# First blocks of a causal self-attention: turned probability tiles laid four to a PSUM bank and copied by whole banks

## The chip, the cores and the metric

The kernel runs on one core of a Trainium2 chip, in one launch. The metric is the device time of that core in microseconds (us): the median of several executions. The engines of a core work side by side, each through its own queue in order, and wait for each other by semaphores: TensorE (PE in the profile, PEld for its weight loads), VectorE (DVE), ScalarE (ACT), GpSimd (POOL) and SyncE (SP, which issues the DMAs). TensorE writes its results to PSUM, which here is eight banks of 128 partitions by 512 float32 values; VectorE and ScalarE take them out of there into SBUF.

## What is computed

The reference is one layer of an encoder and a decoder in float32: model width 512, 16 heads of 32, feed-forward width 2048. The encoder works on 2 x 77 context rows, the decoder on 2 batches of 2048 tokens. Its self-attention is causal, with a bias by relative position:

```python
y = tgt
yn = _ln(y, dec_n1_s, dec_n1_b)
y = y + _mha(yn, yn, dec_sa_in_w, dec_sa_in_b, dec_sa_out_w, dec_sa_out_b, sb)
y = y + _mha(_ln(y, dec_n2_s, dec_n2_b), memory, dec_ca_in_w, dec_ca_in_b, dec_ca_out_w, dec_ca_out_b, cb)
h = _ln(y, dec_n3_s, dec_n3_b)
y = y + (jax.nn.relu(h @ dec_ff1_w.T + dec_ff1_b) @ dec_ff2_w.T + dec_ff2_b)
```

Inside `_mha`, for each head: scores = q k^T / sqrt(32) + bias, softmax over the keys, times the values. `sb` is the bias with minus infinity above the diagonal.

## The kernel before

**Units and visits.** Self-attention is cut by batch `b` (2), block `m` of 512 queries (4), group `g` of four heads (4) and tile `t` of 128 queries (4). One such unit is a row of queries against the key tiles 0 to `i = 4m + t`, so a unit has `i + 1` key tiles of 128. The list `stream` cuts each unit into pieces of up to four key tiles; a visit is one round of the main loop (lines 1811 to 1841), which takes one or two pieces of the same unit. In a first block (`m == 0`) a unit has 1, 2, 3 or 4 key tiles, hence one piece and one visit.

**What a visit issues**, in this order:

- `turn` (lines 412 to 436): the probabilities of the four heads are turned on PE by transposes of 128 x 128 (L426), into a PSUM bank that `bank()` hands out. When a bank has its load, one copy takes it to a buffer of the ring `pts_all` (eight buffers): on ACT (L433) or on DVE (L431). In a first block the loads go by head: four loads, each with the 1 to 4 key tiles of one head. Loads with an even number go to ACT, odd ones to DVE. At the end, `exps` puts the exponentials (L406) of a later unit into ACT's queue.
- `slot(n + 1)`, when the unit ends here: side work for PE and the rest. In first blocks these are projections of q (L215), k (L226 or L1068) and v (L239 or L1068) with their evictions (L217, L231, L242, L1075 to L1093), norms that are turned (L305, taken out by L310 on ACT or L312 on DVE), and stages of another part: in batch 0 the encoder (L577 to L764; among them its scores L606, with the row maxima L616 and sums L627 on DVE), in batch 1 the cross-attention of the very first block (L810 to L882; among them its scores L835 and sums L853).
- `score_next`: the scores of a later unit (L375), four heads into four banks. DVE takes them out (L384 far from the diagonal, L391 with the bias near it), keeping maxima in `mx`; L401 makes the negative row maximum `nm`, for which the exponentials wait.
- `values`: for each key tile and head one matmul of the turned probabilities with the values (L455). It reads the copies in `pts`. In a first block all four tiles of a group add into one bank, which is kept out of the list of banks from the first of them to the last, and is then copied by ACT (L466).

**Banks.** `bank()` hands out the eight banks (seven while one is kept) in a fixed round: the bank just handed out goes to the end of the list. All users draw from the same list: turns, scores, projections, turned norms, side stages. A matmul that writes a bank waits until the engine that empties it has done so.

Of the kernel before, what the change touches and what calls it, by code (L numbers as in the profile page):

```python
# [22 lines left out]
HC = P // HD  # L23
MB = 512
NMB = T // MB
TB = MB // P
# [28 lines left out]
def tile_encoder_decoder(ctx: ExitStack, tc: tile.TileContext, ins, out):  # L55
# [103 lines left out]
    with (  # L159
# [20 lines left out]
        def bank():  # L180

            ring.append(ring.pop(0))
            return psum[:, ring[-1], :]

        def in_turn(what, tile):
            i = count[what] % tile.shape[1]
            count[what] += 1
            return tile[:, i, :]
# [163 lines left out]
        def exps(k):  # L352

            for _ in range(min(k, len(late_exps))):
                late_exps.pop(0)[1]()
# [56 lines left out]
        def turn(pieces):  # L412

            first = units[pieces[0][0]][1] == 0
            loads = []
            for n, k0, kn in pieces:
                ks = range(k0, k0 + kn)
                if first:
                    loads += [[(n, k, r) for k in ks] for r in range(HC)]
                else:  # L420
                    loads += [[(n, k, r) for r in range(HC)] for k in ks]
            for o, load in enumerate(loads):
                pt = bank()
                pts = in_turn("pts", pts_all).rearrange("p (x q) -> p x q", q=P)
                for x, (n, k, r) in enumerate(load):
                    nc.tensor.transpose(pt[:, ts(x, P)], state[n]["p"][r][:, k], ident)  # L426
                    got[n, k, r] = pts[:, x, :]
                w = len(load) * P
                free = pieces[0][0] == len(units) - 2 and pieces[0][1]
                if free or (o % 2 if first else o in (4, 6) if len(loads) == 8 else o >= (len(loads) + 1) // 2):  # L430
                    nc.vector.tensor_copy(pts[:, : len(load), :], pt[:, :w])  # L431
                else:
                    nc.scalar.copy(pts[:, : len(load), :], pt[:, :w])  # L433
                if not first and o == (7 if len(loads) == 8 else min(3, len(loads) - 1)):
                    exps(1)
            exps(HC if first else 0 if units[pieces[0][0]][1] == NMB - 1 else 1)
# [1374 lines left out]
        while i < len(stream):  # L1811
            n = stream[i][0]
# [3 lines left out]
            while any(u == n for u, _ in late_exps):  # L1816
                exps(1)
            ends = pair[-1][1] + pair[-1][2] == size[n]
            turn(pair)
            if n == end - 2:  # L1820
                for _, k0, _ in pair:
# [88 lines left out]
```

## Time and profile before

| | us |
|---|---|
| median of 3 runs | 2738.47 |
| lowest, highest | 2737.07, 2738.86 |
| the profiled execution | 2739.13 |
| its span, first to last instruction | 2737.3 |

| engine | busy us | share of the span | instructions |
|---|---|---|---|
| PE | 2711.1 | 99% | 26462 |
| DVE | 1821.8 | 67% | 5338 |
| ACT | 1539.9 | 56% | 2996 |
| POOL | 991.1 | 36% | 836 |

The granted TensorE clock was 0.999 over the span. The first blocks lie at about 26 to 160 us (batch 0) and 860 to 996 us (batch 1). In these stretches:

```
28.00:160.00 132.00, 126.20 (x1054) 78.54 (x1053) 91.92 (x347) 62.61 (x184) 47.63 (x37) 1.00 0.62 182
860.00:996.00 136.00, 133.46 (x1040) 85.03 (x1030) 90.11 (x340) 74.42 (x214) 46.20 (x41) 1.00 0.46 133
```

The columns are the stretch, its length, the busy time (and number of instructions) of PE, PEld, DVE, ACT and POOL, the granted clock, the share of the DMA engines and GB/s.

How to read the rows further below. A group of instructions has its line, engine, operation, tiles out<-in, shapes and count; then busy us, mean ns of one, and the idle time of the engine before it with what ended it. A row of the timeline has start, length, engine, line, operation and, in brackets, the idle time before it and its releaser. A row of the chain of waits has start, length and what the time is put down to. Matmuls are pipelined: their starts are closer together than their lengths, so what counts for PE is the distance between starts. A wait is put down to the semaphore that came last; an engine is named there that may only have finished at the same moment.

### The profile page before, as it was taken

The page shows a single profiled execution, that of the slowest core. Times are in us where ns is not written, and L with a number is a line of the kernel's source. Part 1 is how long each engine was busy: PE and PEld are TensorE (multiplying, and loading weights), DVE is VectorE, ACT ScalarE, POOL GpSimd, SP SyncE. Part 2 cuts the span into 40 slices and gives each one's busy share as a digit, 9 for nine tenths or more (in the row PEclk, how much of TensorE's full clock was granted, in tenths as well). Part 3 has the DMA queues.
Part 4 walks back from the last instruction along what each step waited for, and adds up shares of the span by engine and source line. Part 5 has one row for each costly group of instructions (what it writes and reads, how often), then busy time and mean ns, then how long its engine had stood idle before and what let it go on. Part 6 is the DMA issues. An engine that isn't in the chain of part 4 may idle for free.

```text
span 2737.3 us, 67718 instructions
## 1 busy us (share of the span) xinstructions
PE 2711.1 (99%) x26462; PEld 2182.6 (80%) x26462; DVE 1821.8 (67%) x5338; ACT 1539.9 (56%) x2996; POOL 991.1 (36%) x836
## 2 busy tenths in 40 slices
PE   9999999999999999999999999999999999999998
PEld 5578777777776677777777887898989898989898
DVE  5776687787875587687787793646464746464645
ACT  3554567767786557667777785444444444444431
POOL 1512234500210513313300103465646564646456
PEclk9999999999999999999999999999999999999999
DMA  7624345511212522333311206565758565756465
GB/s 225 182 86 133 121 126 176 161 55 41 63 48 72 147 75 71 108 111 106 128 44 33 64 19 225 166 220 166 219 166 242 165 219 166 220 166 220 150 224 185
DMA packets 293666, 377.47 MB, mean 138 GB/s; under 512 B 39984, under 2 KB 163936, under 8 KB 293218
## 3 DMA queue, kind: packets, MB, share of 16 engines
q1 hardware_dynamic: 293346, 373.12, 44.3%
q8 instruction: 210, 3.44, 0.5%
q14 instruction: 110, 0.90, 0.1%
HBM read 328.38 MB, written 44.64 MB: 136 GB/s over the span
## 4 chain that ended last, share of the span: by engine, by line
PE 94%; ACT 2%; DVE 2%; issue 1%; POOL 0%; DMA 0%; SPq 0%; ACTq 0%; DVEq 0%; POOLq 0%
PE psum L426 18%; PE psum L1556 14%; PE psum L1585 12%; PE psum L375 11%; PE psum L455 9%; PE psum L1068 8%; PE psum L215 4%; PE psum L1719 3%; PE psum L1676 3%; PE psum L865 2%; ACT pp L406 1%; PE psum L835 1%; PE psum L873 1%; PE psum L589 1%; PE psum L810 1%; PE psum L239 1%
## 5 line engine op out<-in xcount | busy, mean ns | idle before, releaser
L406 ACT ACTIVATE pp<-pp,nm 128x128 f32<-128x128 f32 (+15 forms) x512 | 611.9, 1201 | 30.1 <-DVE nm L401 29.6
L384 DVE TENSOR_SCALAR_CACHE_REDUCE pp<-psum 128x512 f32<-128x512 f32 (+3 forms) x1024 | 556.4, 591 | 56.2 <-PE psum L375 53.7
L433 ACT COPY pts<-psum 128x512 f32<-128x512 f32 (+2 forms) x732 | 383.6, 580 | 277.0 <-PE psum L426 224.8
L426 PE MATMUL psum<-ident,pp 128*128 128x128 f32 x4352 | 527.6, 276 | 9.7 <-ACT nT L310 4.5
L426 PEld LDWEIGHTS psum<-ident,pp 128*128 128x128 f32 x4352 | 471.4, 140 | 67.1 <-DVE pp L384 24.0
L375 PE MATMUL psum<-kT,q 32*128 32x512 f32 (+3 forms) x2560 | 331.7, 560 | 2.8 <-ACT nT L310 1.6
L455 PEld LDWEIGHTS psum<-pts,vv 128*32 128x32 f32 x8704 | 226.6, 110 | 126.5 <-DVE pp L384 47.0
L431 DVE COPY pts<-psum 128x512 f32<-128x512 f32 (+3 forms) x404 | 251.6, 654 | 94.5 <-PE psum L426 92.5
L1585 PE MATMUL psum<-pp 128*128 128x128 f32 x2560 | 304.5, 276 | 1.9 <-POOL pp L961 1.6
L1585 PEld LDWEIGHTS psum<-pp 128*128 128x128 f32 x2560 | 296.3, 192 | 8.6 <-issue 3.0
L455 PE MATMUL psum<-pts,vv 128*32 128x128 f32 x8704 | 278.8, 275 | 0.7 <-DVE mx L391 0.3
L961 POOL TENSOR_TENSOR pp<-pp 128x512 f32<-128x512 f32 x159 | 212.9, 1356 | 121.0 <-DMA pp<-in_dec_ff_wT_dram 45.4
L1556 PE MATMUL psum<-vv,pp 128*128 128x256 f32 x1024 | 236.2, 381 | 0.0
L375 PEld LDWEIGHTS psum<-kT,q 32*128 32x128 f32 x2560 | 142.1, 183 | 106.7 <-issue 42.0
L1556 PEld LDWEIGHTS psum<-vv,pp 128*128 128x128 f32 x1024 | 190.3, 190 | 25.8 <-issue 0.5
L391 DVE CUSTOM_DVE_ANT_0 pp<-psum,bias 128x256 f32<-128x256 f32 (+1 forms) x512 | 196.0, 411 | 20.9 <-PE psum L375 20.8
L1569 DVE TENSOR_TENSOR kT<-kT,psum 128x512 f32<-128x512 f32 x96 | 65.8, 686 | 191.1 <-PE psum L1556 190.9
L1572 ACT ACTIVATE kT<-kT,vecs 128x256 f32<-128x256 f32 x192 | 87.1, 501 | 156.6 <-DVE kT L1569 155.9
L1556 PE MATMUL psum<-nT,pp 128*128 128x256 f32 x768 | 174.1, 380 | 0.0
L1556 PEld LDWEIGHTS psum<-nT,pp 128*128 128x128 f32 x768 | 144.2, 190 | 20.3 <-issue 1.6
L1593 ACT COPY oT<-psum 128x128 f32<-128x128 f32 x56 | 15.0, 268 | 238.8 <-PE psum L1585 238.8
L493 POOL TENSOR_TENSOR oT<-rirows,oT 128x512 f32<-128x512 f32 x30 | 38.4, 1279 | 288.5 <-DMA rirows<-rec 239.9
(257 smaller groups left out, 4049.3 us busy)
## 6 DMA issues: line engine op xcount, KB each, us to landing
pp<-w_d SPq DMA_DIRECT2D x520, 256.0 KB
pp<-in_dec_ff_wT_dram SPq DMA_DIRECT2D x112, 256.0 KB
wqk<-in_dec_sa_in_wT_dram SPq DMA_DIRECT2D x76, 256.0 KB
bias<-tzg SPq DMA_DIRECT2D x128, 128.0 KB
pp<-wo_d SPq DMA_DIRECT2D x56, 256.0 KB
vv<-in_enc_ff_wT_dram SPq DMA_DIRECT2D x8, 1024.0 KB
xr<-in_x_dram SPq DMA_DIRECT2D x32, 256.0 KB
vv<-y SPq DMA_DIRECT2D x32, 256.0 KB
```

The lines of the kernel that those rows point to most:

```text
L375: nc.tensor.matmul(banks[r][:, : kn * P], q[rows4(r), ts(t, P)], kT[rows4(r), g, k0 * P : (k0 + kn) * P], start=True, stop=True,)
L384: nc.vector.tensor_scalar(p[:, k0 : k0 + far], s[:, :far], 1.0, None, ALU.mult, ALU.max, accum_out=st["mx"][:, r, c : c + 1],)
L391: nc.vector.tensor_tensor_reduce(p[:, k0 + far : i + 1], s[:, far:kn], near[:, 2 - (kn - far) :], 1.0, LOWEST, ALU.add, ALU.max, accum_out ...
L406: nc.scalar.activation(p, p, AF.Exp, bias=nm, accum_out=to)
L426: nc.tensor.transpose(pt[:, ts(x, P)], state[n]["p"][r][:, k], ident)
L431: nc.vector.tensor_copy(pts[:, : len(load), :], pt[:, :w])
L433: nc.scalar.copy(pts[:, : len(load), :], pt[:, :w])
L455: nc.tensor.matmul(ot[rows4(r)], vv[:, k, ts(g * HC + r, HD)], got.pop((n, k, r)), start=k == k0 and (whole or not begun), stop=k == k1 - ...
L961: engine.tensor_tensor(out, a, b, ALU.subtract)
L1068: nc.tensor.matmul(mm[:, ts(f, TOK)], left[:, c, ts(f, P)], right[:, c, :], start=c == 0, stop=c == 1,)
L1556: nc.tensor.matmul(mm[:, ts(f, TOK)], a[:, c, ts(f, P)], b[:, c, :], start=fresh and f == 0 and c == 0, stop=c == 1, skip_group_check=True,)
L1585: nc.tensor.matmul(psum[:, bank_i, ts(col, P)], lhs[:, c, :], w[:, c, :], start=fresh and k in (0, 3) and c == 0, stop=c == 3, skip_group_ ...
```

## The change

In `turn`, for first blocks, the loads are no longer one for each head. The turned tiles of a visit are put in one list, head after head, and cut into loads of `TB` = 4:

```diff
                 if first:
-                    loads += [[(n, k, r) for k in ks] for r in range(HC)]
+                    heads = [(n, k, r) for r in range(HC) for k in ks]
+                    loads += [heads[o : o + TB] for o in range(0, len(heads), TB)]
                 else:
                     loads += [[(n, k, r) for r in range(HC)] for k in ks]
```

A visit with 1, 2 or 3 key tiles so has 1, 2 or 3 loads of four tiles instead of 4 loads of 1, 2 or 3 tiles; with 4 key tiles the loads are the same as before. Each load still takes one bank, one buffer of `pts_all` and one copy, even ones on ACT, odd ones on DVE. The transposes keep their order, and the value matmuls theirs.

## The prediction

> **What bounds the kernel now.** I read the page first, then the waits of PE in the two stretches of first blocks (26 to 160 us for batch 0, 860 to 996 us for batch 1), then the timeline and the chain of waits around each of those waits.
>
> ```profile
> span 2737.3 us, 67718 instructions
> ...
> PE 94%; ACT 2%; DVE 2%; issue 1%; POOL 0%; DMA 0%; SPq 0%; ACTq 0%; DVEq 0%; POOLq 0%
> ```
>
> PE carries the chain. What other engines do counts only where PE stands still, so the first question is how long it does in the stretches that the change touches. The waits of PE (who waits, for whom, total us, times, longest), batch 0 first:
>
> ```profile
> PE psum L426 <- ACT nT L310: 3.2, 2, 1.8
> PE psum L426 <- DVE mx L391: 1.1, 2, 0.7
> PE psum L375 <- ACT kT L231: 0.7, 1, 0.7
> PE psum L426 <- ACT pts L433: 0.6, 1, 0.6
> ```
>
> ```profile
> PE psum L426 <- DVE kT L1081: 1.0, 1, 1.0
> ```
>
> Together 6.6 us, the first rows of both answers, nearly all of it at L426: transposes that wait for a PSUM bank in which an older result still stands. That is the most that better use of banks can win directly; every matmul stays as it is.
>
> **The change part by part.** A group of four heads has four visits with 1, 2, 3 and 4 key tiles; two batches of four groups make 8 visits of each size. The fourth is unchanged. The first three make 3 x 4 copies and take as many banks now, and 1 + 2 + 3 = 6 afterwards. Transposes and value matmuls keep their number. The copies, by shape, in 28 to 160 us:
>
> ```profile
> L431 DVE COPY pts<-psum 128x512 f32<-128x512 f32 x8 | 5.3, 686 | 2.9 <-PE psum L426 2.9
> L433 ACT COPY pts<-psum 128x512 f32<-128x512 f32 x8 | 4.7, 586 | 13.1 <-PE psum L426 12.5 <-DVE pts L431 0.6
> ...
> L431 DVE COPY pts<-psum 128x384 f32<-128x384 f32 x8 | 4.1, 548 | 0.0
> L433 ACT COPY pts<-psum 128x384 f32<-128x384 f32 x8 | 3.8, 478 | 12.8 <-PE psum L426 12.0 <-ACT pts L433 0.6
> L433 ACT COPY pts<-psum 128x256 f32<-128x256 f32 x8 | 3.0, 373 | 14.9 <-PE psum L426 14.7
> L431 DVE COPY pts<-psum 128x256 f32<-128x256 f32 x8 | 3.0, 415 | 0.0
> L431 DVE COPY pts<-psum 128x128 f32<-128x128 f32 x8 | 1.9, 280 | 0.0
> L433 ACT COPY pts<-psum 128x128 f32<-128x128 f32 x8 | 1.8, 272 | 1.8 <-PE psum L426 1.8
> ```
>
> Even loads go to ACT, odd ones to DVE. ACT per group: 2 x (0.272 + 0.373 + 0.478) = 2.25 us now, (1 + 1 + 2) x 0.586 = 2.34 us afterwards. DVE: 2 x (0.280 + 0.415 + 0.548) = 2.49 us now, (0 + 1 + 1) x 0.686 = 1.37 us afterwards. Over eight groups ACT does 0.8 us more and DVE 8.9 us less. By itself that is no time: PE sets the end. I cost it at nothing except where a copy stands in the chain, which comes below.
>
> What can move time is which bank a step is given. The list hands out the bank whose last use lies furthest back, so 3, 2 and 1 fewer banks a visit mean that everything after is given an older, more surely emptied bank. I went through the list by the code for both batches, and took at each wait of PE the step that will own the new bank. First the pace of turns without a wait, for 4 and 12 transposes:
>
> ```profile
> 123.28 0.66 PE L426 MATMUL psum<-ident,pp 128*128 128x128 f32 x4
> 123.77 1.89 PE L1068 MATMUL psum<-xt,wqk 128*128 128x256 f32 x8
> ...
> 140.87 1.53 PE L426 MATMUL psum<-ident,pp 128*128 128x128 f32 x12
> ...
> 142.24 1.02 PE L597 MATMUL psum<-vv,pp 128*77 128x512 f32 x2
> ```
>
> The next matmul starts 0.49 us after the first of 4 and 1.37 us after the first of 12: 0.11 us for each transpose, so 0.93 us for 8.
>
> Batch 0, first group, second and third visit:
>
> ```profile
> 33.96 0.88 PE L426 MATMUL psum<-ident,pp 128*128 128x128 f32 x6
> ...
> 35.17 0.41 PE L426 MATMUL psum<-ident,pp 128*128 128x128 f32 x2 [0.34 <-DVE mx L391]
> ...
> 35.64 3.70 PE L226 MATMUL psum<-nT,wqk 128*128 128x512 f32 x8
> ...
> 41.45 1.70 PE L426 MATMUL psum<-ident,pp 128*128 128x128 f32 x12
> ...
> 42.12 0.42 DVE L391 CUSTOM_DVE_ANT_0 pp<-psum,bias 128x256 f32<-128x256 f32 x1
> ...
> 43.29 1.12 PE L239 MATMUL psum<-wbig,nT 128*128 128x512 f32 x2
> ```
>
> The fourth bank of the first turn held head 0's scores. Its two new banks held nothing newer than the visit before. L226 could start at 33.96 + 0.93 = 34.89: 0.75 us won. In the next visit L239 waits for head 1's scores; afterwards it gets the bank of head 0, emptied at 42.54 by the DVE row, so it starts at 41.45 + 1.37 = 42.82: 0.47 us more.
>
> Batch 0, third group, first visit, and batch 1, last group, first visit:
>
> ```profile
> 95.63 0.55 PE L426 MATMUL psum<-ident,pp 128*128 128x128 f32 x3
> ...
> 96.89 0.30 PE L426 MATMUL psum<-ident,pp 128*128 128x128 f32 x1 [0.71 <-DVE mx L391]
> ...
> 97.14 3.70 PE L226 MATMUL psum<-nT,wqk 128*128 128x512 f32 x8
> ```
>
> ```profile
> 961.72 0.44 PE L426 MATMUL psum<-ident,pp 128*128 128x128 f32 x2
> ...
> 963.12 0.67 PE L426 MATMUL psum<-ident,pp 128*128 128x128 f32 x2 [0.97 <-DVE kT L1081]
> ...
> 963.85 1.32 PE L1068 MATMUL psum<-xr,wqk 128*128 128x256 f32 x5
> ```
>
> One bank instead of four: neither turn meets the bank it waits for. 97.14 - (95.63 + 0.49) = 1.02 us and 963.85 - (961.72 + 0.49) = 1.64 us won.
>
> Two waits go without gain. The 0.6 us at L426 in batch 0's second group vanishes, but the chain passes it by:
>
> ```profile
> 79.29 1.43 DVE emx L616
> ...
> 83.71 2.93 ACT pp L406 x8
> 86.64 0.58 ACT kT L231
> ...
> 87.26 0.50 PE psum L375 x8
> ```
>
> DVE and the exponentials set when L375 may start; PE only waits 0.87 us longer there. And the largest, L310 (3.2 us, two waits), stays: the second load of those turns still gets the bank of the turned norm tile that ACT empties behind four exponentials. There the change has a price:
>
> ```profile
> 108.20 1.20 PE L426 MATMUL psum<-ident,pp 128*128 128x128 f32 x9 [1.41 <-ACT nT L310]
> ...
> 109.15 0.48 ACT L433 COPY pts<-psum 128x384 f32<-128x384 f32 x1 [0.65 <-ACT pts L433]
> ...
> 109.53 0.72 ACT L406 ACTIVATE pp<-pp,nm 128x512 f32<-128x512 f32 x1
> ...
> 110.64 0.86 PE L455 MATMUL psum<-pts,vv 128*32 128x128 f32 x24
> ```
>
> ACT's second copy needs 8 transposes after the release instead of 6, 2 x 0.11 us, and is 0.586 - 0.478 = 0.11 us longer. The exponentials behind it, then L310, then the next turn are late by 0.33 us. The value matmuls at 110.64 are not: the copy ends near 110.0. This is the shortest cover of a copy; elsewhere whole projections or encoder stages, as L597 at 142.24, lie between the transposes and L455.
>
> Last, in batch 1's last group the chain runs through DVE's copies themselves:
>
> ```profile
> 977.90 0.93 DVE pts L431 x2
> ```
>
> One copy of 0.69 us there: 0.24 us won.
>
> Sum: 0.75 + 0.47 + 1.02 + 1.64 + 0.24 - 0.33 = 3.8 us. Against the profiled execution, 2739.13 us (span 2737.3 and 1.8 around it), that is 2735.3; that execution lies 0.7 us over the median of 2738.47, so I predict 2734.7 us. After each block PE runs nearly without waits (94% of the chain), so I carry the gain to the end whole; the bounds are nothing carried, and the waits of ACT won as well (rival b).
>
> **The rivals.** (a) *Swallowed.* Each freed wait returns as at 87.26, since DVE or ACT sets the next release. For it: a third of the waits shown behave so. Against: the chain shows PE straight after L226 and L1068. Time: 2738.47 - 0.24 = 2738.2.
>
> (b) *More waits go than I credit.* If DVE's 8.9 us less work and the earlier PE also shorten the ACT waits (3.2 + 0.7 + 0.6 us), 3.8 + 4.5 = 8.3 us are won: 2730.2. For it: DVE stands in the chain at 79.29 and keeps PE at 96.89. Against: those waits end with exponentials that wait for row maxima, and these come before the copies in DVE's order.
>
> (c) *Slower: the late copy delays ACT.* ACT starts a copy only when four transposes are in, and the exponentials queue behind it. By the pace (0.27 us for the first transpose, 0.11 for each more), ACT leaves a first visit's copies at 0.61 + 0.59 = 1.20 us instead of 0.49 + 0.27 = 0.76, and a third visit's at 1.48 + 0.59 = 2.07 instead of 1.15 + 0.48 = 1.63; a second visit's stay. 0.88 us a group, 7.0 us in eight: 2745.5. It decides only where the row maxima are ready before the copies end and PE then waits for ACT; the trace has this once (109.53). [...]
>
> **How the numbers follow.** The forecast has 0.48, (a) 0.12, (b) 0.30, (c) 0.10. A measurement of this kernel tells about 0.2%, 5.5 us, from no change: faster means below 2733.0, slower above 2743.9. All of (b) and an eighth of the forecast's spread are faster, 0.36; of (c) 0.07 is slower; the rest, 0.57, is the same. The range reaches to (b)'s end and past (a): 2730.0 to 2740.0, which leaves out (c) and a deeper (b). The forecast's own range is 2732 to 2737.
>
> **What would show it.** The copies at L431 and L433 fall by 48 in number, all with 128x512 in first blocks. PE's waits at L426 for L391 and for L1081 are gone; those for L310 stay, the second 0.3 us longer. L375's wait for L231 grows to about 1.5 us. PE between 860 and 996 us wins more than between 26 and 160. Wrong would be: a wait at L455 for pts; exponentials released by L433 instead of L401; or any change of more than 1 us after 1000 us, where nothing is touched.

## The result and the profile after

| kernel, set of runs | runs | median us | lowest, highest |
|---|---|---|---|
| before | 15 | 2737.40 | 2735.83, 2738.86 |
| changed, same set | 15 | 2731.85 | 2730.52, 2734.27 |
| changed, second set (before 2737.83) | 11 | 2734.49 | 2732.18, 2736.75 |
| changed, third set (before 2737.87) | 11 | 2734.60 | 2731.46, 2736.86 |

The ratio of the first set is 0.9981, with a 95% interval of 0.9973 to 0.9989: 5.5 us faster, 3.0 to 7.4 us by the interval. The second and third set, which are experiments below, give 0.9987 (0.9978 to 0.9995) and 0.9988 (0.9979 to 0.9997), both 3.3 us. All three intervals hold the 3.8 us of the forecast; why the sets stand 2.6 to 2.8 us apart is a part of the story. In the changed kernel every line from 419 on has a number higher by one (L426 is now L427, L433 is L434, L1068 is L1069).

The page of the changed kernel, its first rows:

```profile
span 2729.1 us, 67656 instructions
...
PE 2706.8 (99%) x26462; PEld 2182.1 (80%) x26462; DVE 1815.2 (67%) x5306; ACT 1539.9 (56%) x2980; POOL 990.0 (36%) x836
```

PE has the same 26462 instructions. DVE has 32 fewer and ACT 16 fewer, which are the 48 copies; DVE is 6.6 us less busy and ACT not at all. (The busy time counts overlapping copies once. By number and mean length, 404 of 654 ns before and 372 of 686 ns after, DVE's copies fall by 9.0 us; the forecast had 8.9.) The waits of PE, batch 0 (26 to 160 us), then batch 1 (857 to 993 us; the columns are total us, times, longest):

```profile
PE psum L427 <- ACT nT L310: 3.0, 2, 1.8
PE psum L375 <- ACT kT L231: 1.4, 1, 1.4
```

```profile
PE psum L375 <- DVE kT L1094: 0.3, 1, 0.3
PE psum L836 <- DVE mx L391: 0.2, 1, 0.2
```

The waits of transposes for L391, for L1081 and for a copy are gone; those for L310 stay, and L375's wait for L231 has doubled, as forecast. The four turns for which the prediction named a gain, by the timeline of PE:

```profile
33.24 1.09 PE L427 MATMUL psum<-ident,pp 128*128 128x128 f32 x8
34.17 2.31 PE L226 MATMUL psum<-nT,wqk 128*128 128x512 f32 x5
```

```profile
39.88 1.53 PE L427 MATMUL psum<-ident,pp 128*128 128x128 f32 x12
41.24 3.17 PE L239 MATMUL psum<-wbig,nT 128*128 128x512 f32 x7
```

```profile
93.17 0.66 PE L427 MATMUL psum<-ident,pp 128*128 128x128 f32 x4
93.66 2.74 PE L226 MATMUL psum<-nT,wqk 128*128 128x512 f32 x6
```

```profile
957.47 0.66 PE L427 MATMUL psum<-ident,pp 128*128 128x128 f32 x4
957.96 2.32 PE L1069 MATMUL psum<-xr,wqk 128*128 128x256 f32 x10
```

No row has a wait in brackets, and the distances between starts are 0.93, 1.36, 0.49 and 0.49 us. Before they were 1.68, 1.84, 1.51 and 2.13 us. So 0.75, 0.48, 1.02 and 1.64 us are gone, 3.9 us in all.

Laid instruction by instruction against the execution before, PE is 0.7 us ahead at 11 us (start-up, where nothing is changed), 2.7 us ahead at 114 us, 5.9 us after batch 1's last group and 8.3 us at the end. Net of the start-up that is 2.0 us in batch 0, 2.9 us in batch 1 and 0.3 us between them. In batch 0 the lead had been 3.75 us and fell to 2.25 us between 108.4 and 110.2 us of the execution before, where the changed kernel ran at half clock (below). The last 2.4 us fall where the two programs are alike: 1.6 us at 1108 to 1112 us, a matter of the clock too, and 0.8 us at 1300 us, where one projection (L1068) waits 0.81 us for its weights from a DMA before the change. Of the fourteen profiles of this document only the two that are by head throughout have such a wait there (0.8 and 1.0 us; at most 0.2 us in the others); whether the change removes it is not shown.

Batch 1 won more than the 1.64 us at its largest wait. The rest is in small holds. Before, and then after:

```profile
899.21 1.09 PE L426 MATMUL psum<-ident,pp 128*128 128x128 f32 x8
900.38 0.63 PE L810 MATMUL psum<-ident,kT 128*128 128x128 f32 x4
...
913.08 0.48 PE L375 MATMUL psum<-kT,q 32*128 32x128 f32 x2 [0.40 <-ACT nT L310]
...
959.57 1.20 PE L375 MATMUL psum<-kT,q 32*128 32x256 f32 x8
```

```profile
896.02 1.09 PE L427 MATMUL psum<-ident,pp 128*128 128x128 f32 x8
896.95 0.60 PE L811 MATMUL psum<-ident,kT 128*128 128x128 f32 x4
...
909.61 0.48 PE L375 MATMUL psum<-kT,q 32*128 32x128 f32 x2 [0.16 <-ACT nT L310]
...
955.82 0.71 PE L375 MATMUL psum<-kT,q 32*128 32x256 f32 x8
```

From the transposes to L811 it is 0.93 us instead of 1.17, the wait inside L375 is 0.24 us shorter, and eight scores take 0.71 us instead of 1.20: 0.97 us in three places. Only one of the three shows as a wait in the list.

### The profile page after: what moved, and what is told of

Its sections match the earlier page's. It is cut to its first block, busy times and chain, and to the rows that moved or that the text cites. A ratio compares the mean times of both kernels' runs of the same rounds, so it can differ in the third digit from the quotient of the medians.

```text
span 2729.1 us, 67656 instructions
## 1 busy us (share of the span) xinstructions
PE 2706.8 (99%) x26462; PEld 2182.1 (80%) x26462; DVE 1815.2 (67%) x5306; ACT 1539.9 (56%) x2980; POOL 990.0 (36%) x836
## 3 DMA queue, kind: packets, MB, share of 16 engines
q8 instruction: 209, 3.42, 0.5%
## 4 chain that ended last, share of the span: by engine, by line
PE 95%; ACT 2%; DVE 1%; issue 1%; POOL 0%; DMA 0%; SPq 0%; ACTq 0%; DVEq 0%; POOLq 0%
PE psum L427 18%; PE psum L1557 14%; PE psum L1586 13%; PE psum L375 11%; PE psum L456 9%; PE psum L1069 8%; PE psum L215 4%; PE psum L1720 3%; PE psum L1677 3%; PE psum L866 2%; ACT pp L406 1%; PE psum L836 1%; PE psum L874 1%; PE psum L590 1%; PE psum L811 1%; PE psum L239 1%
## 5 line engine op out<-in xcount | busy, mean ns | idle before, releaser
L434 ACT COPY pts<-psum 128x512 f32<-128x512 f32 x716 | 384.7, 594 | 273.5 <-PE psum L427 236.1
L427 PE MATMUL psum<-ident,pp 128*128 128x128 f32 x4352 | 526.4, 276 | 6.9 <-ACT nT L310 4.3
L427 PEld LDWEIGHTS psum<-ident,pp 128*128 128x128 f32 x4352 | 471.2, 140 | 62.9 <-DVE pp L384 24.0
L375 PE MATMUL psum<-kT,q 32*128 32x512 f32 (+3 forms) x2560 | 331.2, 561 | 3.2 <-ACT kT L231 1.4
L456 PEld LDWEIGHTS psum<-pts,vv 128*32 128x32 f32 x8704 | 225.8, 110 | 126.5 <-DVE pp L384 47.0
L432 DVE COPY pts<-psum 128x512 f32<-128x512 f32 x372 | 244.5, 686 | 92.1 <-PE psum L427 90.1
L456 PE MATMUL psum<-pts,vv 128*32 128x128 f32 x8704 | 277.8, 275 | 0.7 <-DVE mx L391 0.3
L375 PEld LDWEIGHTS psum<-kT,q 32*128 32x128 f32 x2560 | 142.0, 183 | 106.9 <-issue 42.6
L391 DVE CUSTOM_DVE_ANT_0 pp<-psum,bias 128x256 f32<-128x256 f32 (+1 forms) x512 | 196.0, 411 | 20.8 <-PE psum L375 20.8
```

Of the source, the lines that this page charges most:

```text
L375: nc.tensor.matmul(banks[r][:, : kn * P], q[rows4(r), ts(t, P)], kT[rows4(r), g, k0 * P : (k0 + kn) * P], start=True, stop=True,)
L391: nc.vector.tensor_tensor_reduce(p[:, k0 + far : i + 1], s[:, far:kn], near[:, 2 - (kn - far) :], 1.0, LOWEST, ALU.add, ALU.max, accum_out ...
L456: nc.tensor.matmul(ot[rows4(r)], vv[:, k, ts(g * HC + r, HD)], got.pop((n, k, r)), start=k == k0 and (whole or not begun), stop=k == k1 - ...
```

## The experiments

Experiments with one batch alone, or with one part alone, have 11 runs of their own beside 33 of the kernel before in their set; an interval is about 2.5 us to either side.

**One batch at a time.**

```diff
-                if first:
+                if first and units[n][0] == 0:
                     ...
+                elif first:
+                    loads += [[(n, k, r) for k in ks] for r in range(HC)]
```

The second kernel has `== 1` in that place.

> The change in batch 0 alone. By the prediction's steps (banks): 0.75 + 0.47 + 1.02 - 0.33 = 1.9 us under the kernel before, and in the profile the waits at L426 for L391 gone, those for L310 kept, L375's wait for L231 at 1.4 us. Rival (the work that DVE is spared, 8.9 us in all, spread evenly over the two batches): half of the measured 5.5 us, 2.8 us.

> The change in batch 1 alone. By the prediction's steps: 1.64 + 0.24 = 1.9 us under the kernel before. By the shifts of PE between the profiles of before and after: about 2.9 us, of which some 1.0 us comes from short waits between 900 and 961 us that the prediction left out. Rival (DVE's spared work): 2.8 us, spread over all four groups.

Batch 0 alone: 2735.41 us, ratio 0.9993 (0.9985 to 1.0002), 2.1 us below before by the medians. Batch 1 alone: 2736.34 us, 0.9993 (0.9984 to 1.0002), 1.2 us below. Neither is told from no change by time alone, nor the expected 1.9 us from the rival's 2.8. The traces do tell that each half works where it should: with batch 0 alone the wait for L1081 in batch 1 is still there (1.0 us), and with batch 1 alone it is gone, while batch 0 keeps its two waits for L391 (1.0 us) and the one for a copy (0.6 us). Each half of the change frees its own waits. Batch 0 alone also has a new wait of 0.7 us (L375, for DVE) and three stretches of half clock in its profile, which was its slowest run.

**Banks, or copies?** The first kernel makes the fewer, larger copies but throws away as many banks of the round as it saves. The second keeps the packed banks and cuts each copy in two halves on the same engine, so that there are more copies than by head in the third visits and as many or fewer in the others.

```diff
+            for _ in range(HC - len(loads) if first else 0):
+                bank()
             for o, load in enumerate(loads):
```

```diff
+                halves = [(0, 2), (2, 4)] if first and len(loads) < HC else [(0, len(load))]
...
-                    nc.scalar.copy(pts[:, : len(load), :], pt[:, :w])
+                    for a, z in halves:
+                        nc.scalar.copy(pts[:, a:z, :], pt[:, a * P : z * P])
```

> The copies of the changed kernel with the round of banks of the kernel before: a first visit takes four banks from the list again and leaves the first one, two or three unused. If the banks make the gain, nearly all is lost: within 1 us of the kernel before, and the waits at L426 for L391 and L1081 are back. If fewer copies and DVE's spared work make it, it stays 4 to 6 us faster.

> The banks of the changed kernel with each of its copies in visits of 1 to 3 key tiles cut in two halves of 256 columns, on the same engine: 96 copies instead of 48. If the banks make the gain, it stays within 1 us of the changed kernel (some 0.2 us more where ACT's copies stand ahead of the exponentials at about 109 us). If the number of copies makes it, half or more of the gain is lost: 2 us or less under the kernel before.

With the banks thrown away: 2738.25 us, ratio 1.0005 (0.9996 to 1.0014). With the halves: 2733.64 us, 0.9986 (0.9977 to 0.9994). The waits of PE in batch 0 and in batch 1, and two turns, of the kernel that throws banks away (its L429 is the transposes' line):

```profile
PE psum L429 <- ACT nT L310: 4.2, 2, 2.3
PE psum L429 <- DVE mx L391: 2.3, 3, 1.2
```

```profile
PE psum L429 <- DVE mx L391: 1.8, 1, 1.8
```

```profile
34.06 0.63 PE L429 MATMUL psum<-ident,pp 128*128 128x128 f32 x4 [0.54 <-DVE mx L391]
...
95.77 0.63 PE L429 MATMUL psum<-ident,pp 128*128 128x128 f32 x4 [1.19 <-DVE mx L391]
```

The waits for L391 are back in the first and the third of the four turns, and a new one of 1.8 us stands at the fourth, in batch 1's last group: with one load only, the thrown-away banks come first and the load gets the youngest bank. With 48 copies fewer, nothing is won. The kernel also goes through the ring `pts_all` as the changed kernel does, so it is not the buffers of that ring that make the gain. But its waits for L391 are longer than those before (2.3 us where 1.1 stood, and 1.8 where L1081's 1.0 stood), so this run alone would leave room for a gain of a microsecond or two by the fewer copies. The halves speak against that. They keep the banks, and of the waits shown before only L310 (3.9 us, the longest 2.3) and L231 (1.4 us) are left. Their time is 1.8 us above the changed kernel's first set and 0.8 and 1.0 us below its two others. So it is the bank round that makes the gain; what the number or length of copies does beside it is too small for these runs to show. That also speaks against rival (c) in this kernel: a first half that leaves earlier won nothing that shows.

**The first visits alone** (one key tile; the others by head):

```diff
-                if first:
+                if first and kn == 1:
                     ...
+                elif first:
+                    loads += [[(n, k, r) for k in ks] for r in range(HC)]
```

> Only visits with one key tile are packed (four tiles to one bank, one copy on ACT); visits with 2 and 3 key tiles as before. By the prediction's steps 1.02 + 1.64 = 2.7 us under the kernel before, with the waits at 96.89 and 963.12 us gone and those at 35.17 and 81.56 us back. If the gain is spread evenly over the saved banks (8 x 3 of 48), half of 5.5: 2.8 us. In the profile the two differ: the first has PE win at two places alone.

2734.92 us, ratio 0.9989 (0.998 to 0.9998): 2.9 us below the before of its set. Waits of batch 0:

```profile
PE psum L429 <- ACT nT L310: 2.8, 2, 1.8
PE psum L429 <- ACT kT L231: 0.8, 1, 0.8
...
PE psum L429 <- ACT pts L436: 0.6, 1, 0.6
```

The two large terms, 1.02 and 1.64 us, both stand at first visits. In this profile neither turn waits (the next matmul starts 0.49 us after each), and by the median most of the gain is there. The time cannot tell the theory's 2.7 us from the rival's 2.8. The wait for a copy (0.6 us) is still there, since it needs the packed second visits, and the projection's eviction L231 now meets the transposes of the visit by head, so that most of the 1.02 us is lost again a visit later: a round that is shifted by a part of the change frees some waits and makes others.

**The third copy on DVE.** The prediction's one price, 0.33 us, was ACT's second copy of a third visit. Here the third load goes to DVE as the second does:

```diff
-                if free or (o % 2 if first else ...
+                if free or ((o > 0 if len(loads) == 3 else o % 2) if first else ...
```

> The changed kernel, with the third load of a visit with 3 key tiles copied by DVE instead of ACT. If ACT's late second copy costs the 0.33 us that the prediction put down, the exponentials at about 109 us start with the row maxima and the second wait for L310 is about 0.7 us shorter; DVE's copies in batch 1's last group are 0.6 us longer on the chain. Time: within 1 us of the changed kernel. If the late copy is no cost, the second wait for L310 stays at 1.8 us.

2732.08 us, ratio 0.998 (0.9971 to 0.9989). The two turns that wait for L310, in this kernel:

```profile
105.91 1.09 PE L427 MATMUL psum<-ident,pp 128*128 128x128 f32 x8 [1.48 <-ACT nT L310]
...
111.17 1.53 PE L427 MATMUL psum<-ident,pp 128*128 128x128 f32 x12 [1.48 <-ACT nT L310]
```

From the first release by L310 to the second it is 5.26 us. The next experiment has the same distance for the changed kernel, 5.98 us, so the copy's leave is worth 0.72 us at this place, as the theory had it. DVE's additional work makes L375 wait 0.3 us longer for L1094 in batch 1 (0.6 us instead of 0.3). In its set the kernel is 2.4 us below the changed one, more than the expected 1 us and more than these two give. The rest goes with the clock: 1 of its 11 runs has a mean clock of 0.998, of the changed kernel's 7, and at 0.999 the medians are 2732.88 and 2733.01 us.

**The changed kernel again, twice.**

> The changed kernel again, with another profile. By the prediction's steps 3.8 us under the kernel before; measured so far 5.5. A second theory for the rest: the granted clock falls to half for single windows of 3.41 us, each costing up to 1.7 us; the profiles so far have 1 such window inside the span (before, at 1108 us), 1 (changed, at 105 us, where PE mostly waits anyway), 3 (batch 0 alone) and 2 (batch 1 alone). If it holds, the window at about 1100 us is missing again here, and the times fall into groups 1.7 us apart. If not, the number of windows has nothing to do with the kernel, and the rest is more waits freed.

> The changed kernel itself once more, beside the kernel before of the same set. It measured 5.5 us below before in one set and 3.3 us below in another. Theory (the gain is 3 to 4 us by the bank round and the rest is half-clock windows of up to 1.7 us that come in some executions and not in others): 3 to 5 us below before, with run times spread over 3 to 5 us. Rival (the first set was right and the second disturbed): 5 to 6 us below. Other rival (the reverse): 3 us or less.

2734.49 and 2734.60 us, as in the table above: 3.3 us below before both times, inside the theory's range of 3 to 5. The stretch of half clock at about 1100 us is missing in the first of the two profiles, as the theory had it, and stands in the second, at 1105 us. Both profiles have the same waits in batch 0. Those of the first of them, and its two turns that wait for L310; then the second of these turns in the kernel before (the first, at 108.20 us, stands in the prediction):

```profile
PE psum L427 <- ACT nT L310: 4.0, 2, 2.2
```

```profile
107.26 1.09 PE L427 MATMUL psum<-ident,pp 128*128 128x128 f32 x8 [1.83 <-ACT nT L310]
...
113.24 2.13 PE L427 MATMUL psum<-ident,pp 128*128 128x128 f32 x9 [2.20 <-ACT nT L310]
```

```profile
113.90 0.33 PE L426 MATMUL psum<-ident,pp 128*128 128x128 f32 x1 [1.81 <-ACT nT L310]
```

PE waits 0.8 us longer for L310 than before the change (1.41 + 1.81 us). Half of it is at the first turn: PE comes there earlier, and ACT sets the end. At the second, the distance between the two releases tells what ACT adds: 113.24 - 107.26 = 5.98 us, against 113.90 - 108.20 = 5.70 us. The late copy costs 0.28 us. In the first profiled execution the second wait was only 1.20 us; there the clock fell to half at 104.9 us, between the two turns, and PE was late itself.

**The norm's evictions on DVE.** The largest wait left is for L310, the turned norm tile that ACT empties behind the exponentials. Two of the four tiles of the block after are taken out by ACT there; this edit gives all four to DVE (L312):

```diff
-                    on = nc.vector if x == 1 and t % 2 else nc.scalar
+                    on = nc.vector if x == 1 else nc.scalar
```

> The changed kernel, with the turned norm tiles of the second block taken out by DVE alone, not by ACT behind four exponentials. If those two waits (3.0 us) are what remains for PE in batch 0's first block, they shrink to 1.5 us or less in total: 1 to 3 us under the changed kernel, more if the half-clock window near 105 to 114 us goes with them. Rival: DVE, busy there, is late with the row maxima instead, and the time stays within 1 us of the changed kernel.

> The changed kernel with all four turned norm tiles of the block's second unit copied on DVE, again, to see whether it is faster than the changed kernel itself when both stand in one set. Theory (the wait for L310 in the first blocks, 3.0 to 4.0 us, shrinks to 0.7 us and no half-clock window follows it): 2 to 3 us below the changed kernel of this set. Rival (the difference of the last set was where the windows fell): within 1 us of it.

2731.51 and 2732.36 us, ratios 0.9978 (0.9969 to 0.9987) and 0.998 (0.9971 to 0.9989): 3.0 and 2.2 us below the changed kernel of the same set. The wait at L427 of the first of them, and the stretch from 102 to 115 us of three kernels, first before, then the changed kernel's second execution, then this one (columns as in the stretches above):

```profile
PE psum L427 <- DVE nT L312: 0.7, 2, 0.4
```

```profile
102.00:115.00 13.00, 9.78 (x110) 7.23 (x107) 10.75 (x56) 10.16 (x29) 7.28 (x6) 1.00 0.23 75
```

```profile
102.00:115.00 13.00, 8.85 (x97) 6.80 (x98) 9.68 (x46) 10.07 (x28) 8.52 (x7) 0.94 0.25 83
```

```profile
102.00:115.00 13.00, 11.57 (x100) 7.35 (x100) 11.66 (x48) 9.01 (x28) 9.40 (x7) 1.00 0.17 56
```

PE is busy for 11.57 us of 13 instead of 8.85, at full clock instead of 0.94. This is the fastest of the kernels that stand in more than one set. Part of that is the clock again: at a mean clock of 0.999 it is 1.7 and 1.2 us below the changed kernel of its set.

**The same edit on the kernel before, and both ACT edits together.**

> The kernel before, its probability tiles copied by head as they were, with the turned norm tiles on DVE as in the run above. It tells whether that edit needs the change. Theory (the wait for L310 is a matter of its own, 3.2 us in before): 2 to 3 us below before, the waits for L391 and L1081 still there. Rival (by head, the waits for L391 take the place of L310 and PE stands as long): within 1 us of before.

> The changed kernel with both edits that relieve ACT: the turned norm tiles on DVE, and the third copy of a visit of three loads on DVE. Theory (after the first edit the wait for L310 is nearly gone, so the second has only the 0.3 us of ACT's late copy to give and takes 0.3 us at L375 for L1094): within 1 us of the kernel with the norm tiles alone. Rival (DVE becomes the bound with both, its queue ahead of the row maxima too long): 1 us or more above it, with longer waits of PE for L391 or L1094.

By head: 2737.05 us, ratio 0.9998 (0.999 to 1.0007), 0.8 us below before. Its first waits in batch 0:

```profile
PE psum L426 <- DVE mx L391: 1.2, 3, 0.7
PE psum L426 <- DVE nT L312: 1.1, 2, 0.6
```

L310's 3.2 us became 1.1 us at L312, yet the time hardly moved: the rival's side, though the interval reaches to 2.7 us and does not exclude the theory. With both edits on the changed kernel: 2733.63 us, 0.9986 (0.9977 to 0.9995), 1.3 us above the norm tiles alone. The waits for L312 and for L1094 are 1.3 and 0.6 us instead of 1.0 and 0.3. By the median that is the rival's side; the waits explain 0.6 us of the 1.3, and the rest is within the spread of runs. ACT's copies are not worth moving a second time.

## Why the prediction was right

**The sum.** 0.75, 0.47, 1.02 and 1.64 us came out as 0.75, 0.48, 1.02 and 1.64 us. They were read from the distance between starts, at the pace of turns without a wait, and from who owns the new bank in the round; that pace is the one PE took. That the bank round is the mechanism is shown by the kernel that throws the saved banks away and loses the gain, together with the halves, which keep the banks and the gain.

**The swallowed wait.** The 0.6 us at L426 in batch 0's second group went, and came back a stage later, as said; the estimate was 1.5 us:

```profile
84.95 0.50 PE L375 MATMUL psum<-kT,q 32*128 32x128 f32 x8 [1.37 <-ACT kT L231]
```

**The 0.24 us of DVE's copy in the chain** was mis-sized. The chain of waits before and after, where the row maxima of batch 1's last group end and the next stage starts on DVE:

```profile
977.70 0.02 DVE mx L391
977.72 0.02 issue
977.74 0.16 DVE nm L401
...
978.83 0.40 DVE pp L842
```

```profile
971.79 0.02 DVE mx L391
971.81 0.04 issue
971.86 0.96 PE psum L836 x24
972.82 0.47 DVE pp L843
```

From the end of L391 to the next stage it was 1.11 us, through DVE's copies. Now it is 1.01 us, and PE's scores L836, which need L391's banks, end last. The copy became 0.24 us shorter, but only 0.10 us of it counted.

**The price of 0.33 us** for the late copy was right (0.28 us). What was left out beside it is 0.4 us at the first wait for L310: rival (a) in one place, an earlier PE that meets the same ACT. The second wait for L310 was to be 0.3 us longer: it is 0.4 us longer in two profiles of the changed kernel, and 0.6 us shorter in the first, where PE came late.

**What the sum did not have.** The 0.97 us of small holds in batch 1 were left out, since the prediction went by the first rows of the list of waits. And there was no term for the clock. So it is partly luck that the second and third set (2734.49 and 2734.60 us) lie within 0.3 us of the forecast of 2734.7: the mechanism and the four large terms were right, but the holds left out (0.97 us) and what the clock took back (about 1 us, next) happen to be of one size.

**The clock.** Each run's mean granted clock stands with its time. Grouped by it, over the three sets of before (99 runs), the three of the changed kernel (37) and the two with the norm tiles on DVE (22), number of runs and median us:

| granted clock | before | changed | changed, norm tiles on DVE |
|---|---|---|---|
| 1.000 | 43: 2736.70 | 5: 2731.42 | 4: 2731.76 |
| 0.999 | 54: 2738.30 | 16: 2733.01 | 15: 2731.34 |
| 0.998 | 2: 2739.90 | 16: 2734.91 | 3: 2734.29 |
| all | 99: 2737.64 | 37: 2733.35 | 22: 2731.68 |

At the same clock the changed kernel is 5.3, 5.3 and 5.0 us faster; at 0.999 within the second and the third set it is 5.2 and 5.4 us. What the 1.5 us above the forecast's 3.8 are made of is shown only in part: 0.97 us of holds, less 0.5 us for the wait at L310 and the copy in the chain. Over all runs the changed kernel is 4.3 us faster, since it runs at 0.998 in 16 of 37 runs and the kernel before in 2 of 99. By this grouping about 1 us of the gain is lost to the clock. Much of the difference between the sets is the same thing: 4 of 15 runs of the first set are at 0.998, and 7 and 5 of 11 in the two others. Not all of it: at 0.998 the first set's median is 2733.68 us and the second's 2735.53. That rest stays open; the second set's profile is 1.4 us later than the first's already at 10 us, where nothing is changed.

**The rivals.** (a) holds in two places, at L375 and at the first wait for L310. (b) does not: the ACT waits grew. (c) holds only at the one place that the sum had priced (0.28 us): nothing at L456 waits for a copy, and cutting the copies wins nothing. Of the signs named as "wrong", one appeared, a change of more than 1 us after 1000 us. For 1.6 of the 2.4 us it is the clock: the kernel before had a stretch of half clock there (0.50 from 1108.40 to 1111.81 us), and the profiled execution of the changed kernel had none. In the third set the changed kernel had one too, at 1105 us. The other 0.8 us are the wait for a DMA at 1300 us.

## What to carry to other kernels

Where all results draw on one round of PSUM banks, a step that takes fewer banks is paid for by its successors (here 3.9 us won at four turns): read the gain from who owned the bank that each of them will now get, and from the distance between starts, and not from the number of copies saved. Look also at the holds that are too short for a list of waits; here they were a quarter as large as the listed gain (0.97 of 3.9 us). Once the waits on one engine are freed, look at what PE meets next: here it was ACT's evictions of the norm. To move those measured 2 to 3 us after the banks had been freed and 0.8 us before, where the intervals do not yet tell the two apart.

## What was not expected of the hardware

The TensorE clock falls to half for a single short stretch, in the middle of a kernel that keeps PE busy 99% of its span. The clock column (third from the right) of the kernel before, then of the changed kernel:

```profile
1100.00:1105.00 5.00, 5.00 (x46) 4.46 (x44) 3.80 (x12) 4.71 (x12) 3.53 (x5) 1.00 0.30 109
1105.00:1110.00 5.00, 4.89 (x49) 3.17 (x50) 4.89 (x25) 4.03 (x9) 2.78 (x3) 0.84 0.47 125
1110.00:1115.00 5.00, 5.00 (x64) 4.45 (x60) 2.04 (x6) 3.57 (x7) 1.64 (x2) 0.82 0.63 193
```

```profile
105.00:110.00 5.00, 5.00 (x51) 4.11 (x49) 3.06 (x15) 3.67 (x11) 0.00 (x0) 0.67 0.02 5
```

In the first fence 0.16 x 5 + 0.18 x 5 = 1.7 us of PE's work are lost, which at half clock is a stretch of 3.4 us; the clock is 0.50 from 1108.40 to 1111.81 us, 3.41 us. In the second, 0.33 x 5 = 1.65 us; there it is 0.50 from 104.93 to 108.34 us. The medians of before and of the changed kernel in the table above stand 1.6 to 1.9 us apart from one clock to the next, about what one such stretch costs. The mean clock counts the stretches only roughly, because every profile also ends in 0.3 to 3.4 us of half clock: at 0.999 the profiles have none, one or two stretches ahead of that end, at 0.998 two or three. With batch 0 alone the clock falls at 87.3 and at 107.8 us, 20.5 us or six such lengths apart.

In the profiles such stretches lie mostly at two places. One is 105 to 117 us, where PE stands for L310. Of ten profiles in which these waits remain, seven have a stretch of half clock there: the changed kernel in all three (at 104.9, 113.3 and 112.1 us), and the kernels with one batch, with the banks thrown away and with the halves. The kernel before, the one with first visits alone and the one with the third copy on DVE have none. The four profiles with the norm tiles on DVE have none. All four profiles with a wait of 2.2 us or more have it, and three of the six with shorter ones. That the waits for L310 bring it fits all of this, but no experiment changed the waits alone. The length of the longest wait alone does not tell it: 1.8 us stand in three profiles with such a stretch and in two without. The 3.42 us ahead of the fall and the 3.41 us from it on, in the changed kernel's second execution, then 3.41 us with the least work of PE between 100 and 120 us before the change:

```profile
109.93:113.35 3.42, 1.22 (x25) 0.79 (x18) 1.71 (x12) 3.42 (x11) 0.78 (x1) 1.00 0.02 5
113.35:116.76 3.41, 3.41 (x14) 2.89 (x15) 1.40 (x3) 1.82 (x7) 3.33 (x4) 0.50 0.00 0
```

```profile
111.69:115.10 3.41, 1.60 (x15) 1.36 (x14) 1.50 (x10) 2.65 (x9) 1.79 (x2) 1.00 0.01 5
```

In the seven profiles PE is busy for only 1.17 to 1.60 us of the 3.41 us ahead of the fall. In the kernel before, the 1.60 us were not followed by one: the clock is 1.00 from 115.10 to 118.51 us too. Of the six others without a fall there, the one with first visits alone also has a wait of 1.8 us; in the other five no wait for L310 or L312 is longer than 1.48 us. So PE did not stand still throughout ahead of a fall, and how little work goes with one stays open (with batch 0 alone the clock also fell at 87.3 us, where PE is busy for 7.89 of the 10 us from 80 to 90).

The other place is 1104 to 1112 us, in seven of the fourteen profiles, where PE waits for nothing: in the first row above it is busy 5.00 of 5.00 us, in the second 4.89, and the clock falls at 1108.4 us. Idle time as the profile counts it does not explain that one; the same program had it in one execution and not in another. The 3.41 us ahead of it hold almost only scores L375 (32*128 in the rows, where the transposes have 128*128): sixteen of them start at 1104.32 us, and the next line at 1108.30. But the changed kernel's first execution has the same sixteen from 1098.38 to 1102.36 us, and its clock is 1.00 there and from 1100 to 1120 us. What sets it stays open too.
